# Where SyncE loads the rows of x and the tokens' values in a one-core cross-attention kernel

## The chip, the cores and the metric

The kernel runs on one core of a Trainium2 chip. The metric is the device time of one execution in microseconds. A core has TensorE (PE; its weight loads are listed as PEld), VectorE (DVE), ScalarE (ACT), GpSimd (POOL) and SyncE (SP). SP computes nothing here: it issues DMA transfers, one after the other in program order, and a transfer whose condition is not met holds up all transfers behind it on SP. POOL can issue transfers too, in its own order between its computations.

## The reference, cut to what matters

16 batches of 100 rows of x (640 wide), and for each a context of 722 rows (384 wide), of which the last 4 are extra tokens.

```python
query, keyt, valt = hidden_states @ Wq, enc @ Wk, enc @ Wv     # enc: 718 context rows
hs = _mha(query, keyt, valt)                                   # 8 heads of 80
ca_q1 = jnp.einsum('btc,th->bch', ca, Wq_ca)[:, indices, :]    # ca: the 4 tokens
ca_hs1 = _mha(ca_q1, residual, residual)                       # residual is x
ca_hs2 = _mha(ca_hs1 @ Wq, ca @ Wk_ca, ca @ Wv_ca)
out = (hs + ca_hs2) @ Wout + b_out + residual
```

So each row of the output needs, besides the main attention `hs`, a second small attention over the four tokens, whose values are `ca @ Wv_ca`, and at the very end the row of x itself.

## The kernel before, in words

Before the loop the kernel computes what all batches share. Among this are the tokens' values for all 64 tokens, written to a table `va_d` in DRAM (lines 1310 to 1327).

The loop (line 1346) goes over batches b = 0 to 15 and is software-pipelined. The order of all instructions on every engine is the order of the source (`manual_schedule`, line 1345); tiles come from pools with a fixed number of buffers, and the waits follow from who wrote and who read a buffer last. For batch b it runs, in TensorE's order:

- scores of b against the 718 keys (`s_ps`, line 716), three groups; ScalarE copies them to `st`, and DVE folds them into a running maximum `most` (lines 1392 and 1380). The last of these instructions is kept under the name `seen` (line 1401);
- a small product for the tokens' attention (`z_ps`, line 934);
- keys of batch b+1 and values of batch b from the context (`k_ps`, `v_ps`, lines 465 and 434). They are made by a scheme with fewer products: a bank of PSUM is filled, read by DVE or ScalarE (lines 405 and 407), and filled on top, so TensorE waits for these readings. `Maximum` (line 791) meanwhile turns `most` into one maximum per row: transpose (807), reductions, `spread` on ScalarE (829), transpose to `over` (837). Then `st - over` on DVE (1368) and the exponential on ScalarE (1376);
- the last fifth of the keys (`kT_ps`, 666); in some batches the output product (`o_ps`) of earlier rows or the queries of the next pair (`q_ps`);
- the product with V (`a_ps`, line 1585), 192 pairs of weight load and matmul in the trace, and the tokens' product `y_ps` (880) for a later batch. Then the next batch's scores.

The second attention is `Second` (line 859), mostly on POOL: `scores1` (four products and three sums of 100 x 800, waiting for `seen`), `scores2` (973), `softmax3` (987) and `values2` (line 992: `hs2`, the four tokens' values weighted, lines 1002 and 1009). For `values2` each of the four rows of `va_d` is spread over 100 partitions into a tile `vb` (250 KB); there are two such buffers. Tokens 0 and 1 are loaded by `Second.load`, **issued by POOL** (line 951, called at 1387, 1462, 1503 and 1559); tokens 2 and 3 by SP, each when the product on the buffer before it is done (line 1013).

`Last` (line 1023) finishes output rows. The 1600 rows are cut into 13 groups (`OC`). `Last.load` (line 1031) has SP load the rows of x of a finished group into `xn` (320 KB for 128 rows), and POOL adds the bias in place (1042). Pairs of groups are loaded in batches 3, 6, 8, 11 and 13 (line 1463). In the last batch three groups remain: `last.load()` (1531) for 128 rows and for 64 rows in two halves, `mine.load()` (1532) for the last 128 rows in a tile `spare`. `project_few` (1200) then multiplies the 64 rows by Wout, and DVE adds the result to `xn` (1213); the bigger groups follow at lines 1128 and 1122.

SP's order around the end of a batch is: tokens 2 and 3 (956); the next queries' rows and `ca` (203, 870); three loads of the context of batch b+2 (219); `mb` (843); two more of the context, `rest` (232), which wait for the last key product; then, in the batches named, `xn` (1041). As nothing holds these, they are issued while the product with V of the batch before runs.

Of the kernel before, what the change touches and what calls it, by code (L numbers as in the profile page):

```python
# [126 lines left out]
def kernel(  # L127
# [18 lines left out]
    nc = tc.nc  # L146
# [131 lines left out]
    for g in range(2):  # L278
        for c in range(CC):
            nc.scalar.dma_start(  # L280
                out=wv_sb[:, 2 * c + g],
                in_=wv[c * P : (c + 1) * P, g * (H // 2) : (g + 1) * (H // 2)],
# [42 lines left out]
    for h, c, r, s, k in PIECES:  # L325
        nc.gpsimd.dma_start(
            out=m2[s : s + k, c, h - HEADS[c][0], :T],
            in_=wqcat[h * D + r : h * D + r + k, :],
# [4 lines left out]
    for c in range(HC):  # L333
        first = c * P - HEADS[c][0] * D
        nc.gpsimd.affine_select(
            out=hmask[:, c], in_=hmask[:, c], compare_op=ALU.is_ge, fill=0.0,
# [3 lines left out]
            out=hmask[:, c], in_=hmask[:, c], compare_op=ALU.is_ge, fill=0.0,  # L340
# [439 lines left out]
    def wait_for(ins, other):  # L780

        tc.add_manual_dep(
            ins.ins,
            other.ins.name,
            mybir.DependencyInfo(
                mybir.DependencyClass.Sync, mybir.DependencyReason.DATA
            ),
            reason="apart",
        )
# [69 lines left out]
    class Second:  # L859
# [87 lines left out]
            )  # L947
            self.z = z

        def load(self):  # L950
            self.vb = [self.piece(nc.gpsimd, t) for t in range(2)]

        def piece(self, engine, t):
            b = self.b
            vb = vb_tile(f"vb_{b}_{t}")
            engine.dma_start(
                out=vb[:S], in_=va_d[b * T + t].unsqueeze(0).to_broadcast([S, H])
            )
            return vb

        def scores2(self, engine=nc.vector):
# [61 lines left out]
    class Last:  # L1023
# [4 lines left out]
            self.split = b == B - 1  # L1028
            self.t_ps = None

        def load(self):

            self.xn = {}
            for r, (lo, n) in enumerate(OC):
                if self.b != O_AFTER[r]:
                    continue
                xn = self.xn[r] = spare[1] if r == len(OC) - 1 else xn_tile(f"xn_{r}")
                rows = x.rearrange("b s n -> (b s) n")[lo : lo + n]
                for at, cols in self.parts(n):
                    to = xn[at : at + n, : cols.stop - cols.start]  # L1040
                    nc.sync.dma_start(out=to, in_=rows[:, cols])
                    nc.gpsimd.tensor_tensor(to, to, bias[at : at + n, cols], ALU.add)

        def parts(self, n):
# [201 lines left out]
    for n, heads in enumerate(HEADS):  # L1246
        cols = len(heads) * B * T
# [26 lines left out]
    second = Second(0, xT, ca_0)  # L1274
# [71 lines left out]
    for b in range(B):  # L1346
        p = b // 2
        e_in, now = enc, second
# [35 lines left out]

        if b == 0:
            enc_sums(enc)
            now.load()
            now.softmax1()
        st.append(scores(b, 0, tiles))
        if b == 0:  # L1390
# [15 lines left out]
        if b == 0:  # L1406
            second.scores1()
            m_next = load_m(b + 2)
            kk.go(3)
            top.go(3)  # L1410
            first_values(3, e_in, (act, act), get=bank)
            top.go(1)
            kk.go(2)
            now.scores2()
            now.exponentials2()
            first_values(0, e_in, (act, act), (0,), bank)
            top.go()
            kk.go(3)
            first_values(0, e_in, (act, act), (1,), bank)
            now.softmax3()  # L1420
            kk.go(2)
            subtract(0)
            exponential(0)
            kk.go(2)
            subtract(1)
            kk.go(3)
            exponential(1)
            second_next, enc_next = loads()
            less = subtract(2)
            exponential(2)  # L1430
            last_keys(b + 1, enc)
            enc_next = load_rest(b + 2, enc_next)
            keys(m_next)
            now.values2(less)
            enc_sums(enc_next)
            second.softmax1(4)
        elif b + 1 < B:
            vv = Values(b, e_in)

            def both(n):  # L1440
                vv.go(n)
                kk.go(n)

            forms = [wout_sb[:, 2 * i : 2 * i + 2, k * (H // 2) : (k + 1) * (H // 2)]
                     for i in range(2) for k in range(2)]
            if b == 2:
                for o, left, right in (
                    (forms[1], forms[1], forms[0]),
                    (wout2[:, 0], forms[3], forms[1]),
                    (wout2[:, 1], forms[2], wout2[:, 0]),  # L1450
                ):
                    nc.gpsimd.tensor_tensor(o, left, right, ALU.subtract)
            elif last.b - 1 in PAIRS:
                nc.gpsimd.tensor_tensor(wout2[:, 0], wout2[:, 0], forms[0], ALU.add)
            second.scores1(seen, range(T - 1))
            top.go(3)
            kk.go(3)
            vv.go(3)
            now.scores2(nc.gpsimd)
            second.scores1(None, range(T - 1, T))  # L1460
            if b == 1:
                now.load()
            last.load()
            top.go(1)
            if b > 1:
                last.place()
            now.exponentials2()
            both(2)
            both(2)
            top.go()  # L1470
            both(1)
            now.softmax3()
            if b == 1:
                nc.gpsimd.tensor_tensor(last.hs[:S], last.hs[:S], last.hs2, ALU.add)
            if last.b in PAIRS:
                last.sums()
            parted = b % 2 and b > 1 and last.b not in PAIRS
            now.values2(None, range(T - 1 if parted else T))
            vv.go(2)
            kk.go(1)  # L1480
            subtract(0)
            exponential(0)
            vv.go(1)
            subtract(1)
            vv.go(1)
            kk.go(2)
            exponential(1)
            vv.go(1)
            kk.go(2)
            both(1)  # L1490
            both(1)
            if b == 1:
                for f in list(wv_there):
                    nc.scalar.copy(wv_sb[:, W_AT[f]], wv_there.pop(f))
            mixed = None
            if b % 2 and b > 1:
                second_next, enc_next = loads()
                mixed = Queries(p + 1, xT_at[0], enc_next[0])
            if parted:
                mixed.sums()  # L1500
                now.values2(None, range(T - 1, T))
            else:
                second.load()
            if b == 1:
                nc.gpsimd.dma_start(out=bias, in_=bout[0].partition_broadcast(P))
            if not mixed:
                second_next, enc_next = loads()
            if b + 2 < B:
                m_next = load_m(b + 2)
            subtract(2)  # L1510
            exponential(2)
            last_keys(b + 1, enc)
            if b + 2 < B:
                enc_next = load_rest(b + 2, enc_next)
            if b == 1:
                last.transpose()
            if last.b in PAIRS:
                second.softmax1(3)
                last.project_pair()
                if last.b == max(PAIRS):  # L1520
                    nc.sync.dma_start(
                        out=forms[1],
                        in_=wout[: 2 * P, H // 2 :].rearrange("(c p) n -> p c n", p=P),
                    )
            second.softmax1(3 if parted else 8)
        else:
            room = enc_tile("spare").rearrange("p f k -> p (f k)")
            spare.extend(room[:, i * H : (i + 1) * H] for i in range(2))
            last.transpose()
            vv = Values(b, e_in)  # L1530
            last.load()
            mine.load()
            top.go(3)
            vv.go(3)
            last.project_few(len(OC) - 2)
            now.scores2(nc.gpsimd)
            now.exponentials2()
            top.go(1)
            vv.go(2)
            top.go()  # L1540
            vv.go(3)
            now.softmax3()
            now.values2()
            vv.go(2)
            subtract(0)
            exponential(0)
            vv.go(5)
            for i in (1, 2):
                subtract(i)
                exponential(i)  # L1550
            last.project()
        if b % 2 and b + 1 < B:
            xT, tiles = xT_at[0], queries_tiles(p + 1)
            if not mixed:
                for n in range(HC):
                    queries(p + 1, xT, tiles, n)
            elif parted:
                mixed.make(tiles, second.softmax1)
                second.load()
            else:  # L1560
                keys(m_next)
                mixed.sums()
                mixed.make(tiles, second.softmax1)
# [109 lines left out]
```

## Time and profile before

| what | value |
|---|---|
| device time, median of 3 runs | 924.46 us (923.11 to 924.51) |
| device time of the profiled execution | 922.65 us |
| its span, first to last instruction | 920.9 us |
| granted TensorE clock | 1.000 |
| transfers issued by POOL for `vb` | 32 |
| transfers issued by SP for `vb` | 32 |
| bytes moved, mean rate | 62.94 MB, 68 GB/s |

The profile is one execution, recorded instruction by instruction. In its timeline a row has the start and length in us, the engine, the source line, the operation, the tile written, the tiles read, shapes and the number of instructions merged; in brackets is the idle time of the engine before it and what ended it. A row of the table of windows has a stretch of time, its length, the busy time of each engine in it with the number of instructions, the granted clock, the busy share of the 16 DMA engines and the rate. Line numbers are those of the kernel before.

### The profile page before, as it was taken

To read this page: it belongs to the slowest core of one execution; us is meant where nothing else is said; L and a number is where in the kernel's file an instruction comes from. 1 tells how busy PE (TensorE), PEld (TensorE's weight loads), DVE (VectorE), ACT (ScalarE), POOL (GpSimd) and SP (SyncE) were. 2 spreads that over 40 slices of the span, in tenths; PEclk is the share of its full clock that TensorE was granted. 3 is DMA by queue.
4 is the path that set the end of the run, shared out by engine and by line. 5 is a ranking of instruction groups with operands and counts; after the bars stand their busy time and mean duration, and the time that the engine had idled before them with its cause. 6 is when DMAs were issued, how large, how long until landed. Compare 5 with 4: busy or idle time off the path is not lost.

```text
span 920.9 us, 27684 instructions
## 1 busy us (share of the span) xinstructions
PE 911.9 (99%) x11974; PEld 766.2 (83%) x11974; DVE 692.5 (75%) x1116; ACT 434.4 (47%) x836; POOL 723.6 (79%) x689
## 2 busy tenths in 40 slices
PE   9999999999999999999999999999999999999998
PEld 6988879787797979888798887988879888797966
DVE  3469895988649887795967869689784898748883
ACT  2234543737427373552737436264741737426341
POOL 5849999788977879697896969958798687976623
PEclk9999999999999999999999999999999999999999
DMA  8722013050300404031030410205030050310201
GB/s 270 269 77 78 25 49 95 1 156 2 104 32 11 119 1 134 3 97 60 24 111 3 117 40 30 77 2 155 3 101 33 2 157 1 104 46 3 81 23 38
DMA packets 49681, 62.94 MB, mean 68 GB/s; under 512 B 14072, under 2 KB 38200, under 8 KB 49560
## 3 DMA queue, kind: packets, MB, share of 16 engines
q1 hardware_dynamic: 45512, 51.49, 18.3%
q0 software_dynamic: 3024, 8.53, 3.0%
q8 instruction: 94, 1.54, 0.7%
q10 hardware_dynamic: 1024, 1.15, 0.4%
q14 instruction: 27, 0.22, 0.1%
HBM read 55.59 MB, written 5.57 MB: 66 GB/s over the span
## 4 chain that ended last, share of the span: by engine, by line
PE 97%; DVE 1%; DMA 0%; POOL 0%; issue 0%; ACT 0%; SPq 0%; ACTq 0%; POOLq 0%
PE s_ps L716 12%; PE a_ps L1585 11%; PE v_psA L434 11%; PE v_psB L434 9%; PE k_psA L465 8%; PE kT_ps L666 8%; PE k_psB L465 7%; PE o_ps L1160 5%; PE v_psC L434 4%; PE k_psC L465 3%; PE v_ps L375 2%; PE q_ps L593 2%; PE q_ps L535 2%; PE v_psD L434 2%; PE v_psE L434 2%; PE q_psA L593 1%
## 5 line engine op out<-in xcount | busy, mean ns | idle before, releaser
L905 POOL TENSOR_TENSOR e<-ca,g 100x800 f32<-100x800 f32 x64 | 99.4, 1564 | 91.8 <-ACT kT L407 64.3
L500 POOL TENSOR_TENSOR enc<-enc 128x240 f32<-128x240 f32 x135 | 106.6, 800 | 18.2 <-DMA enc<-in_enct 11.1
L1368 DVE TENSOR_TENSOR st<-st,over 120x1600 f32<-120x1600 f32 x48 | 113.8, 2373 | 0.0
L1585 PEld LDWEIGHTS a_ps<-vs,st 120*36 120x36 f32 (+3 forms) x3072 | 109.4, 124 | 3.9 <-issue 3.1
L1585 PE MATMUL a_ps<-vs,st 120*36 120x81 f32 (+3 forms) x3072 | 111.9, 233 | 0.3 <-ACT st L1376 0.3
L434 PE MATMUL v_psA<-wv_sb,enc 128*120 128x320 f32 x352 | 109.3, 433 | 0.0
L1009 POOL TENSOR_TENSOR hs<-hs,hs 100x640 f32<-100x640 f32 x48 | 96.3, 2007 | 3.8
L912 POOL TENSOR_TENSOR e<-e,e 100x800 f32<-100x800 f32 x48 | 92.1, 1919 | 3.8
L1002 POOL TENSOR_TENSOR hs<-vb,p 100x640 f32<-100x640 f32 x64 | 90.3, 1421 | 3.7 <-DMA vb<-va_d 0.9
L434 PE MATMUL v_psB<-wv_sb,enc 128*120 128x320 f32 x296 | 91.8, 433 | 0.0
L465 PE MATMUL k_psA<-enc,wk_sb 128*128 128x240 f32 x360 | 89.2, 370 | 0.0
L1376 ACT ACTIVATE st<-st 120x1600 f32<-120x1600 f32 x48 | 73.9, 1539 | 30.9 <-DVE st L1368 30.5
L434 PEld LDWEIGHTS v_psA<-wv_sb,enc 128*120 128x120 f32 x352 | 64.2, 183 | 25.0 <-DVE vs L405 0.5
L465 PEld LDWEIGHTS k_psA<-enc,wk_sb 128*128 128x128 f32 x360 | 67.2, 190 | 15.1
L1380 DVE TENSOR_TENSOR most<-most,st 120x800 f32<-120x800 f32 x64 | 67.3, 1052 | 15.5 <-ACT st L766 14.4
L716 PE MATMUL s_ps<-qp,kT 64*56 64x100 f32 (+1 forms) x3072 | 73.7, 248 | 0.6 <-issue 0.6
L465 PE MATMUL k_psB<-enc,wk_sb 128*128 128x240 f32 x300 | 73.0, 366 | 0.0
L716 PEld LDWEIGHTS s_ps<-qp,kT 64*56 64x56 f32 (+1 forms) x3072 | 67.1, 130 | 6.4 <-issue 5.2
L434 PEld LDWEIGHTS v_psB<-wv_sb,enc 128*120 128x120 f32 x296 | 54.1, 183 | 21.9 <-DVE vs L405 0.4
L1075 ACT COPY hsT<-turned_hs 32x160 f32<-32x160 f32 (+7 forms) x244 | 67.7, 278 | 3.0
L772 ACT COPY st<-s_ps 120x800 f32<-120x800 f32 x64 | 49.8, 829 | 34.3 <-PE s_ps L716 34.3
L465 PEld LDWEIGHTS k_psB<-enc,wk_sb 128*128 128x128 f32 x300 | 57.0, 190 | 7.7
(200 smaller groups left out, 1864.7 us busy)
## 6 DMA issues: line engine op xcount, KB each, us to landing
vb<-va_d POOLq DMA_DIRECT2D x32, 250.0 KB, 3.6
vb<-va_d SPq DMA_DIRECT2D x32, 250.0 KB
enc<-in_enct SPq DMA_DIRECT2D x30, 240.0 KB
enc<-in_enct SPq DMA_DIRECT2D x15, 360.0 KB
xT<-in_xt SPq DMA_DIRECT2D x8, 500.0 KB
rest<-in_enct SPq DMA_DIRECT2D x31, 120.0 KB
xn<-in_x SPq DMA_DIRECT2D x11, 320.0 KB
out<-xn SPq DMA_DIRECT2D x11, 320.0 KB
```

The source lines that it names most:

```text
L434: nc.tensor.matmul(at[0][j][:KN, : H // 2], a_form(self.enc, f)[:, j * KN : (j + 1) * KN], wv_there.get(f, wv_sb[:, W_AT[f]]), start=first ...
L465: nc.tensor.matmul(at[:, i * KT : (i + 1) * KT], wk_sb[:, W_AT[f], i], a_form(self.enc, f), start=(first and i == 0), stop=last, skip_grou ...
L500: nc.gpsimd.tensor_tensor(out, left, right, op)
L666: nc.tensor.matmul(bank[:, i * KT : (i + 1) * KT], weights[c], a_raw(enc, u, c), start=(i == 0 and c == 0), stop=(c == CC - 1), skip_group ...
L716: nc.tensor.matmul(s_ps[at][k0:k1, cols], w, rhs, start=not begun & {(at, k) for k in range(k0, k1, 32)}, stop=last, skip_group_check=True,)
L905: first = nc.gpsimd.tensor_tensor(to, self.ca[:, t, :].unsqueeze(1).to_broadcast([S, NH, S]), g[:, :, t].unsqueeze(2).to_broadcast([S, NH, ...
L912: nc.gpsimd.tensor_tensor(e, e, to, ALU.add)
L1002: first = nc.gpsimd.tensor_tensor(to, self.vb[t][:S].rearrange("p (h d) -> p h d", h=NH), p2[:, :, t].unsqueeze(2).to_broadcast([S, NH, D] ...
L1009: nc.gpsimd.tensor_tensor(sums, sums, to, ALU.add)
L1368: return nc.vector.tensor_tensor(st[i], st[i], top.over[:KN].unsqueeze(1).to_broadcast([KN, 2, ROWS]), ALU.subtract,)
L1376: nc.scalar.activation(st[i], st[i], AF.Exp, scale=SCALE)
L1585: nc.tensor.matmul(a_v[lo:hi, h % 4], st[i // 2][: KEYS[i], i % 2, h * S + lo : h * S + hi], block(i, h // 4)[: KEYS[i], h % 4], start=(i ...
```

## The change

The tokens' values of tokens 0 and 1 are issued by SP and not by POOL (POOL keeps batch 0), and in the batch that uses them instead of in the batch before. The first of them, and in batches 1 to 14 the rows of x as well, get a wait on `seen`, the last maximum over that batch's scores. In the last batch the rows of x get no wait of their own; their place in SP's order is behind the tokens' values. The bias addition keeps its place in POOL's order, and no computation is added or removed.

```diff
-        def load(self):
-            self.vb = [self.piece(nc.gpsimd, t) for t in range(2)]
-
-        def piece(self, engine, t):
+        def load(self, engine=nc.sync, behind=None):
+            self.vb = [self.piece(engine, t, behind) for t in range(2)]
+
+        def piece(self, engine, t, behind=None):
             b = self.b
             vb = vb_tile(f"vb_{b}_{t}")
-            engine.dma_start(
+            dma = engine.dma_start(
                 out=vb[:S], in_=va_d[b * T + t].unsqueeze(0).to_broadcast([S, H])
             )
+            if behind:
+                wait_for(dma, behind)
             return vb
...
-        def load(self):
+        def load(self, behind=None):
...
-                    nc.sync.dma_start(out=to, in_=rows[:, cols])
+                    dma = nc.sync.dma_start(out=to, in_=rows[:, cols])
+                    if behind:
+                        wait_for(dma, behind)
                     nc.gpsimd.tensor_tensor(to, to, bias[at : at + n, cols], ALU.add)
...
-            now.load()
+            now.load(nc.gpsimd)
...
-            if b == 1:
-                now.load()
-            last.load()
+            now.load(behind=seen)
+            last.load(seen)
...
-            else:
-                second.load()
             if b == 1:
                 nc.gpsimd.dma_start(out=bias, in_=bout[0].partition_broadcast(P))
...
             vv = Values(b, e_in)
+            now.load(behind=seen)
             last.load()
             mine.load()
...
                 mixed.make(tiles, second.softmax1)
-                second.load()
```

## The prediction

> **What bounds the kernel now.** I read the page first: busy times, DMA queues, then the chain that ended last.
>
> ```profile
> PE 911.9 (99%) x11974; PEld 766.2 (83%) x11974; DVE 692.5 (75%) x1116; ACT 434.4 (47%) x836; POOL 723.6 (79%) x689
> ...
> q8 instruction: 94, 1.54, 0.7%
> ...
> PE 97%; DVE 1%; DMA 0%; POOL 0%; issue 0%; ACT 0%; SPq 0%; ACTq 0%; POOLq 0%
> ```
>
> TensorE carries 97% of the chain, so no transfer is worth its own length: the change counts only where it alters a stall of TensorE. Batches repeat the same instructions, so stalls show when one stage is compared across batches. The table of windows does it, from the first product with V (a_ps) to the first key product after the next batch's scores. Columns: stretch, length, busy time (instructions) of PE, PEld, DVE, ACT, POOL, clock, DMA share, GB/s. The rows are the products of batches 2, 4, 10 and 12.
>
> ```profile
> 195.50:212.33 16.83, 15.78 (x518) 14.62 (x517) 11.88 (x23) 6.58 (x12) 12.68 (x19) 1.00 0.35 91
> 309.39:324.60 15.21, 15.21 (x518) 14.35 (x517) 11.03 (x22) 5.83 (x11) 12.69 (x19) 1.00 0.22 59
> 636.54:652.73 16.19, 15.42 (x517) 14.41 (x516) 11.43 (x22) 5.83 (x11) 11.78 (x19) 1.00 0.31 95
> 749.79:765.43 15.64, 15.47 (x517) 14.41 (x516) 11.37 (x21) 5.85 (x11) 12.02 (x19) 1.00 0.31 96
> ```
>
> Batch 4 has no idle time (15.21 of 15.21). Batches 2, 10 and 12 lose 1.62, 0.98 and 0.43 us. The timeline says where, with the idle time in brackets:
>
> ```profile
> 204.38 1.25 PE L716 MATMUL s_ps<-qp,kT 64*56 64x100 f32 x46 [0.47 <-issue]
> ...
> 211.95 0.45 PE L934 MATMUL z_ps<-y_sb,e 100*32 100x33 f32 x31 [0.58 <-issue]
> ...
> 644.73 0.52 PE L880 MATMUL y_ps<-m,xT 128*64 128x108 f32 x8 [0.77 <-POOL enc L500]
> ...
> 758.02 1.43 PE L716 MATMUL s_ps<-qp,kT 64*64 64x100 f32 x56 [0.17 <-issue]
> ```
>
> Three are "issue": waiting for nothing the profile shows. I take them for the loading of TensorE's own instructions. Queue q8 moved 1.54 MB in 94 packets, 16 KB each; 2 x 11974 TensorE instructions over 94 are 255 per packet. In this stage some 518 + 517 pass in 15.21 us: a packet is used up in 3.75 us, and the next must be there. Here are the transfers around batch 10's product: timeline, windows of 1 us, and the DMA view of 642.25 to 643.40 (packets, MB, share).
>
> ```profile
> 635.93 1.10 POOL L956 DMA_DIRECT2D vb<-va_d  x2
> ...
> 636.64 0.82 SPq L232 DMA_DIRECT2D rest<-in_enct  x2
> ...
> 637.51 0.90 SPq L1041 DMA_DIRECT2D xn<-in_x  x2
> ```
>
> ```profile
> 639.00:640.00 1.00, 1.00 (x35) 1.00 (x32) 0.96 (x2) 0.00 (x0) 0.62 (x1) 1.00 0.94 311
> ...
> 641.00:642.00 1.00, 1.00 (x34) 1.00 (x31) 0.97 (x3) 0.19 (x1) 0.48 (x1) 1.00 1.01 389
> ...
> 643.00:644.00 1.00, 0.96 (x28) 0.81 (x23) 0.79 (x3) 0.00 (x0) 1.00 (x3) 1.00 0.00 0
> ```
>
> ```profile
> q8 instruction: 1, 0.02, 5.4%
> ```
>
> The DMA engines are full (0.94 to 1.01) until just after 642; only as they empty does the instruction packet pass, and 1.3 us after that view's end TensorE resumes. Batches 2, 10 and 12 are those in which vb, rest and xn all load at the product's start. Batch 4 has vb and rest but no xn, share 0.22, and no stall. So I put 644.73 down to the same cause, not to POOL, which the wait names.
>
> **Part 1: loads out of the product.** vb (2 x 250 KB) and xn (2 x 320 KB) leave this stretch; rest stays. All 1.62 + 0.98 + 0.43 = **3.0 us** should go, the second stall of batch 2 being a consequence of the first. Bounds: 0 if rest alone delays the packet; 4.8 if the 1.81 us by which the median (924.46) exceeds the profiled execution (922.65) are stalls of this kind too. I take 3.0, the rows' own value.
>
> [...]
>
> **Part 2: POOL gives up 30 of its 32 issues.**
>
> ```profile
> L956 POOL DMA_DIRECT2D vb<-va_d x32: 537/555/627, 72.2 to 863.0; - x32
> ...
> DMA to landing us min/median/max: 3.2/3.6/5.4
> ```
>
> 30 x 0.555 = 16.7 us of POOL work go, worth nothing beyond Part 1: the only in-loop stall of TensorE on POOL is the 0.77 us counted there. SP takes the 30 issues, about 0.4 us each; it has the time:
>
> ```profile
> SPq L956 <- POOL hs L1002: 509.7, 32, 41.5
> ```
>
> **Part 3: the new wait, batches 1 to 14.** `seen` is the last maximum over the scores; the transpose of `most` follows it. SP now holds vb until then; behind vb stand xn, the tokens 2 and 3, and the next loads. The last two groups were already held by later work. Batch 11:
>
> ```profile
> 655.88 1.01 DVE L807 STREAM_TRANSPOSE turned<-most 128x800 f32<-128x800 f32 x1
> ...
> 668.27 3.05 POOL L1042 TENSOR_TENSOR xn<-xn,bias 128x640 f32<-128x640 f32 x2
> ```
>
> POOL first wants xn 12.4 us after `seen`, being busy with the next scores, and vb later still. Loads that need some 6 us (below) are hidden: 0 us. If that cover were gone, the whole 6 us would show. They now run beside key and value products, where an instruction packet lasts over 20 us (four value products, 888.03 below, take 1.24).
>
> **Part 4: the last batch, where the cover is gone.** There is no next batch, so POOL is idle. xn, its two halves and the last rows carry no wait there, but SP's order puts them behind vb, which waits. Before, they were loaded during batch 14:
>
> ```profile
> 850.78 1.53 SPq L956 DMA_DIRECT2D vb<-va_d  x2
> 852.40 1.60 SPq L1041 DMA_DIRECT2D xn<-in_x  x3
> ```
>
> ```profile
> 856.50:857.00 0.50, 0.50 (x4) 0.41 (x3) 0.49 (x2) 0.00 (x0) 0.49 (x1) 1.00 0.04 13
> 857.00:858.00 1.00, 1.00 (x6) 0.78 (x6) 1.00 (x2) 0.00 (x0) 1.00 (x1) 1.00 0.00 0
> ```
>
> The same five loads took from 850.78 to about 856.7, 5.9 us. What they release, across the engines:
>
> ```profile
> 863.54 3.33 POOL L1042 TENSOR_TENSOR xn<-xn,bias 128x640 f32<-128x640 f32 x3
> 866.95 1.55 POOL L1042 TENSOR_TENSOR spare<-spare,bias 128x640 f32<-128x640 f32 x1
> 886.17 0.24 POOL L973 TENSOR_TENSOR e<-s,mx 100x32 f32<-100x32 f32 x1 [17.68 <-DVE mx L971]
> 893.97 2.51 POOL L1002 TENSOR_TENSOR hs<-vb,p 100x640 f32<-100x640 f32 x2
> ```
>
> ```profile
> 878.74 2.01 DVE L1380 TENSOR_TENSOR most<-most,st 120x800 f32<-120x800 f32 x2
> ...
> 884.88 0.49 DVE L1213 TENSOR_TENSOR xn<-o_ps,xn 128x320 f32<-128x320 f32 x1 [0.64 <-issue]
> ...
> 886.15 0.82 DVE L405 TENSOR_TENSOR vs<-v_psA,vs 120x640 f32<-120x640 f32 x1
> ...
> 888.32 1.01 DVE L837 STREAM_TRANSPOSE over<-spread 128x800 f32<-128x800 f32 x1 [0.35 <-ACT spread L829]
> ...
> 896.95 0.82 DVE L405 TENSOR_TENSOR vs<-v_psB,vs 120x640 f32<-120x640 f32 x1 [0.30 <-PE v_psB L434]
> ```
>
> ```profile
> 886.58 1.71 ACT L829 COPY spread<-mx 64x800 f32<-64x800 f32 x2
> ```
>
> ```profile
> 888.03 1.24 PE L434 MATMUL v_psA<-wv_sb,enc 128*120 128x320 f32 x4
> ...
> 897.88 1.29 PE L1109 MATMUL o_ps<-wout_sb,hsT 128*128 128x320 f32 x4
> ```
>
> `seen` is 878.74 + 2.01 = 880.75. The five loads are issued from 880.8. In batch 14 the second vb came 1.2 us after the first; here it comes 0.4 after, 0.8 sooner, so they land at X between 880.8 + 5.1 and + 5.9; I take **X = 886.5**. (Outer bounds: the fifth is issued about 882.6, two vb at 0.4 and xn's parts at 0.5 later than 880.8, and a vb load took 3.2 to 5.4 us: 885.8 to 888.0.) POOL then adds the bias: 3.33 us, so DVE L1213, which reads those rows, starts at X + 3.4 = 889.9, not 884.88. POOL's fourth addition ends at X + 5.0; L973 stands behind it, 891.5 instead of 886.17. ScalarE's exponential waits for L973 and stands ahead of the spread; `over` came 888.32 - 886.17 = 2.15 us after L973, so it comes at X + 7.2 = 893.7: **+5.4 us** (4.7 to 6.9). DVE executes in order: behind `over` stand the readings of the value banks (L405), the first subtraction, and the reading at 896.95 that frees a bank for the o_ps product at 897.88. TensorE cannot refill a bank before DVE reads it, so DVE's short waits for TensorE in this run shift too. Nothing absorbs the 5.4 us, and all that follows the o_ps product shifts by it. vb itself, wanted at 893.97, is in time.
>
> **The sum:** 922.65 - 3.0 + 0 + 5.4 = **925.05 us** against the profiled execution (span 920.9 plus 1.75 around it). On the median, 1.81 us higher, it is 924.46 + 2.4 = **926.9 us**.
>
> **Rivals**, on the median. *More stalls than the profile holds:* the runs' extra 1.81 us are instruction stalls too, the gain is 4.8, the sum +0.6: 925.1. For it: the run times scatter over 1.4 us; against it: eleven products show none. *Faster:* the same mechanism further. It decides from a gain of 5.4 + 1.85 = 7.3 us, so from about four more stalls of 1.0 us (the mean of 1.62, 0.98 and 0.43): -1.9, 922.5. Against it: that exceeds the 1.81 us. *No gain:* rest and the context loads hold the instruction packet as long, and only the tail counts: 924.46 + 5.4 = 929.9. For it: rest is issued within 0.9 us of the others; against it: batch 4. [...] *A slower clock:* TensorE's product at 888.03 waits for the reading at 886.15, which comes 5.0 us later and ends at 892.0: 4.0 us idle. If the clock then halves for the two products that TensorE can do before DVE sets the pace again, 1.24 us each, up to 2.5 us are added: 929.4. The rows shown have clock 1.00 throughout, and no such gap. [...] *The change not doing what it says* has no chance of its own: the 30 loads stand in SP's order.
>
> **How the numbers follow.** A measurement can tell about 0.2% (1.85 us) from no change. Forecast 926.9: 0.42. More stalls, within 0.2%: 0.30. Faster: 0.13. No gain: 0.10. Clock: 0.05. Slower is 0.42 + 0.10 + 0.05 = 0.57. The range goes from -1.0 us (gain 6.4; beyond it lies most of "faster") to the no-gain case, 923.5 to 929.9, and leaves out less than 0.2. The forecast alone, X from 885.8 to 888.0, spans 926.2 to 928.4.
>
> **What would show it.** Windows of the products of batches 2, 10 and 12 at 15.2 us show Part 1; at 15.6 to 16.8, "no gain". POOL L1042 in batch 11 waiting for DMA breaks Part 3. In the last batch, POOL L1042 some 5.8 us after `seen` and waiting for DMA, `over` 12.9 us after `seen` (7.6 now), and a TensorE gap of about 4 us after the v_psE product show Part 4; L1213 at its old distance from `seen` (4.1 us) would make the forecast wrong.

## The result and the profile after

| | before | after |
|---|---|---|
| device time, median of 15 runs each | 923.11 us (920.39 to 925.47) | 928.04 us (924.62 to 930.85) |
| the profiled execution | 922.65 us, span 920.9 | 924.62 us, span 922.9 |
| granted TensorE clock of the profiled execution | 1.000 | 0.998 |

The ratio is 1.0051, 95% interval 1.0036 to 1.0066. A second set of runs of the same kernel (below, e7) gave 926.85 against 923.92 us, 1.0031 (1.0014 to 1.0047). The change makes the kernel slower by 0.3 to 0.5%.

The page of the kernel after, busy times. It says little: POOL has 30 instructions and 18.8 us less (723.6 before), and TensorE's busy time is the same.

```profile
PE 911.7 (99%) x11974; PEld 766.2 (83%) x11974; DVE 701.6 (76%) x1116; ACT 434.5 (47%) x836; POOL 704.8 (76%) x659
```

The stages say more. Table of windows of the kernel after, the products with V of batches 2, 10 and 12 (the row of batch 4, 15.21 us as before, is not shown):

```profile
194.74:209.95 15.21, 15.21 (x517) 14.35 (x517) 12.14 (x22) 5.82 (x11) 11.96 (x18) 1.00 0.10 25
...
634.12:649.33 15.21, 15.21 (x517) 14.35 (x516) 11.18 (x22) 5.82 (x11) 11.94 (x18) 1.00 0.09 23
746.42:761.63 15.21, 15.21 (x517) 14.35 (x517) 11.17 (x22) 5.82 (x11) 11.96 (x18) 1.00 0.09 22
```

Length equals PE's busy time in all of them: the stalls of 1.62, 0.98 and 0.43 us are gone, and the DMA share fell from about 0.33 to 0.10. The last batch gives back more than that. Timeline of the kernel after (line numbers moved by a few: L1384 was L1380, L1046 was L1042, L1217 was L1213, L1113 was L1109):

```profile
874.71 2.01 DVE L1384 TENSOR_TENSOR most<-most,st 120x800 f32<-120x800 f32 x2
876.79 0.73 SPq L956 DMA_DIRECT2D vb<-va_d  x2
877.88 1.57 SPq L1043 DMA_DIRECT2D xn<-in_x  x3
...
883.15 3.27 POOL L1046 TENSOR_TENSOR xn<-xn,bias 128x640 f32<-128x640 f32 x3 [24.74 <-DMA xn<-in_x]
886.46 0.49 DVE L1217 TENSOR_TENSOR xn<-o_ps,xn 128x320 f32<-128x320 f32 x1 [6.26 <-POOL xn L1046]
...
887.59 0.81 DVE L405 TENSOR_TENSOR vs<-v_psA,vs 120x640 f32<-120x640 f32 x1
...
888.46 1.84 PE L434 MATMUL v_psA<-wv_sb,enc 128*120 128x320 f32 x4 [4.30 <-DVE vs L405]
...
890.15 1.01 DVE L837 STREAM_TRANSPOSE over<-spread 128x800 f32<-128x800 f32 x1 [0.82 <-ACT spread L829]
...
900.10 5.60 PE L1113 MATMUL o_ps<-wout_sb,hsT 128*128 128x320 f32 x20
```

`seen` is 874.71 + 2.01 = 876.72. Read the chain by its brackets: SP issues the loads behind `seen` (vb, xn, and spare right after); POOL, idle for 24.74 us, waits for the DMA; DVE waits 6.26 us for POOL; TensorE waits 4.30 us for DVE's reading of v_psA. From `seen` to the o_ps product it is now 23.38 us; before it was 897.88 - 880.75 = 17.13: **+6.25 us**. The same four product matmuls at 888.46 take 1.84 us and not 1.24, and the table of windows shows why in its PEclk column (the first of the last three):

```profile
888.00:890.00 2.00, 1.54 (x4) 1.05 (x5) 1.23 (x2) 1.71 (x3) 0.24 (x2) 0.79 0.36 82
890.00:892.00 2.00, 2.00 (x5) 1.27 (x4) 1.78 (x3) 0.12 (x1) 0.00 (x0) 0.50 0.00 0
892.00:894.00 2.00, 2.00 (x7) 1.26 (x7) 1.92 (x5) 0.75 (x2) 0.00 (x0) 0.86 0.00 0
```

The clock drops to half behind the gap, for (0.21 x 2 + 0.50 x 2 + 0.14 x 2) / 0.50 = 3.4 us. It sets in at 890.00 - 0.21 x 2 / 0.50 = 889.16, 0.7 us after TensorE has resumed.

Part 3 of the prediction is seen in batch 11, same kernel, timeline: vb is issued at `seen` (652.46) and xn 0.8 us behind it, and POOL's addition, 12.4 us after `seen` as before, has no bracket, so it waits for nothing.

```profile
653.28 0.83 SPq L1043 DMA_DIRECT2D xn<-in_x  x2
...
664.88 3.04 POOL L1046 TENSOR_TENSOR xn<-xn,bias 128x640 f32<-128x640 f32 x2
```

### The profile page after: what moved, and what is told of

Same layout as the page of the kernel before. It is cut to its first block, busy times and chain, and to the rows that moved or that the text cites. A ratio compares the mean times of both kernels' runs of the same rounds, so it can differ in the third digit from the quotient of the medians.

```text
span 922.9 us, 27705 instructions
## 1 busy us (share of the span) xinstructions
PE 911.7 (99%) x11974; PEld 766.2 (83%) x11974; DVE 701.6 (76%) x1116; ACT 434.5 (47%) x836; POOL 704.8 (76%) x659
## 4 chain that ended last, share of the span: by engine, by line
PE 97%; DMA 1%; DVE 1%; POOL 0%; issue 0%; ACTq 0%; SPq 0%; POOLq 0%
PE s_ps L716 12%; PE a_ps L1586 12%; PE v_psA L434 10%; PE v_psB L434 9%; PE k_psA L465 8%; PE kT_ps L666 8%; PE k_psB L465 7%; PE o_ps L1164 5%; PE v_psC L434 4%; PE k_psC L465 3%; PE v_ps L375 2%; PE q_ps L593 2%; PE q_ps L535 2%; PE v_psD L434 2%; PE v_psE L434 2%; PE q_psA L593 1%
## 5 line engine op out<-in xcount | busy, mean ns | idle before, releaser
L1380 ACT ACTIVATE st<-st 120x1600 f32<-120x1600 f32 x48 | 73.9, 1539 | 32.0 <-DVE st L1372 31.3
L1384 DVE TENSOR_TENSOR most<-most,st 120x800 f32<-120x800 f32 x64 | 65.9, 1030 | 16.6 <-ACT st L766 15.5
```

What stands on the lines that cost most here:

```text
L1380: nc.scalar.activation(st[i], st[i], AF.Exp, scale=SCALE)
```

## The experiments

The theory: the loss is the last batch's wait alone, and the loop gains some 3 to 4 us. The rival: moving the loads costs something inside batches 1 to 14 as well. e1 and e2 separate the two halves of the change; e3 and e4 split its gain; e5, e8 and e9 test what makes a stall; e6 and e7 size the tail. Times are medians, each beside runs of the kernel before on the same chip.

**e1, the rows ahead of the values.** The changed kernel with one line of the last batch moved:

```diff
-            now.load(behind=seen)
             last.load()
             mine.load()
+            now.load(behind=seen)
```

> The changed kernel, but in the last batch the rows of x stand ahead of the tokens' values in SP's order, as they did before the change. Theory, that the loss is the last batch's wait: L1217 and `over` come as long after `seen` as before (4.1 and 7.6 us), TensorE has no idle time of 4 us and stays at clock 1.000, and the gains in the loop remain: 3.8 to 4.5 us faster than the kernel before, 918.5 to 919.5 us against a median of 923.1. Rival, that waits or transfers inside batches 1 to 14 cost what was gained in the products: the run stays within 1 us of the changed kernel, 927 to 928. Between them, 921 to 922: the gain of 4.3 us that the two profiles show is larger than what the other executions have.

Measured: 919.83 against 923.49 us, 0.9966 (0.9953 to 0.9978), 3.7 us faster than the kernel before. Timeline of e1:

```profile
875.86 2.00 DVE L1384 TENSOR_TENSOR most<-most,st 120x800 f32<-120x800 f32 x2
...
881.97 0.49 DVE L1217 TENSOR_TENSOR xn<-o_ps,xn 128x320 f32<-128x320 f32 x1 [0.61 <-issue]
...
894.97 5.60 PE L1113 MATMUL o_ps<-wout_sb,hsT 128*128 128x320 f32 x20
```

L1217 starts 4.1 us after `seen` (877.86), as before, and the o_ps product 17.11 us after it (17.13 before): the tail is back to what it was. The rival inside the loop falls. The stalls are not quite zero here: products of batches 2 and 4 took 15.57 and 15.72 us, with waits of TensorE called "issue", and rest the only one of the three loads beside them.

**e2, the last batch alone.** The kernel before, with only this: the load in batch 14 is left to the last batch, and goes to SP there (not shown: `load` takes the engine and the wait as arguments, as in the change).

```diff
-            else:
+            elif b < B - 2:
                 second.load()
...
             vv = Values(b, e_in)
+            now.load(nc.sync, seen)
             last.load()
```

> The kernel before, with only the last batch as in the change: SP loads tokens 0 and 1 behind `seen`, ahead of the rows of x. Theory, that the wait of the last batch costs about 6 us by itself and the drop of the clock behind it 1 to 2 us more: 6 to 8 us slower than the kernel before, 929 to 931, with the stalls in the products of batches 2 and 10 still there and one stretch of half clock behind a TensorE gap of about 4 us. Rival, that the wait is hidden as long as the loop keeps its old order: within 1 us of the kernel before, 922 to 924.

Measured: 930.77 us, 1.0083 (1.0069 to 1.0098). Its products of batches 2, 10 and 12 keep their stalls (windows), and its tail is that of the kernel after (timeline):

```profile
194.59:210.69 16.10, 15.77 (x518) 14.62 (x517) 11.12 (x22) 6.03 (x12) 11.79 (x19) 1.00 0.33 95
...
635.74:651.60 15.86, 15.42 (x518) 14.42 (x517) 10.92 (x22) 5.83 (x11) 11.89 (x19) 1.00 0.33 97
749.01:764.91 15.90, 15.47 (x517) 14.41 (x516) 11.06 (x22) 5.85 (x11) 12.02 (x19) 1.00 0.33 96
```

```profile
878.00 2.01 DVE L1382 TENSOR_TENSOR most<-most,st 120x800 f32<-120x800 f32 x2
...
889.71 0.49 DVE L1215 TENSOR_TENSOR xn<-o_ps,xn 128x320 f32<-128x320 f32 x1 [6.21 <-POOL xn L1044]
...
903.35 2.91 PE L1111 MATMUL o_ps<-wout_sb,hsT 128*128 128x320 f32 x10
```

Its loop is that of the kernel before up to batch 13, so the two profiles show how far one execution can be trusted: batches 2, 4, 10 and 12 took 16.83, 15.21, 16.19 and 15.64 us there and 16.10, 15.72, 15.86 and 15.90 here. The stall of a single product is known to some 0.7 us only.

From `seen` (880.01) to o_ps 23.34 us, +6.21. The two halves add up: -0.34% (e1) and +0.83% (e2) make +0.49%, and the whole change was measured at +0.51 and +0.31%.

**e3, the rows alone,** and **e4, the values alone.** The kernel before, with one of the two groups of loads held until `seen`. e3 leaves the last batch as it was (not shown: the argument of `Last.load`, as in the change). e4 has the load function of the change and its place in the loop, and the last batch of e1, where the rows stand ahead of the values:

```diff
-            last.load()
+            last.load(seen)
```

> The kernel before, with only the rows of x held until `seen` in batches 1 to 14; the tokens' values stay on POOL and in the product. Theory, that what holds up TensorE's instructions is the sum of transfers started at the head of the product, of which the rows are the largest: the products of batches 10 and 12 fall to 15.2 us, 1.4 to 3 us faster than before, about 920 to 921.5, no gap in the last batch. Rival, that the tokens' values are what delays the instructions (or POOL's issues): the products keep 16.2 and 15.6 us and the time stays within 0.7 us of before.

```diff
-            if b == 1:
-                now.load()
             last.load()
+            now.load(behind=seen)
```

> The kernel before, with only the tokens' values moved to SP and held until `seen`; the rows of x are loaded as before, ahead of them in SP's order, in the last batch too. Theory, that the sum of transfers at the head of a product decides and not one of them: the products of batches 2, 10 and 12 lose most of their stalls, 1.4 to 3.5 us faster than before, 919.5 to 921.5, no gap in the last batch. Rival, that the rows alone fill the DMA engines long enough: the products of batches 10 and 12 keep their 16.2 and 15.6 us, only batches 0 to 2 gain, 1 to 2 us.

Measured: e3 921.17 us, 0.9979 (0.9969 to 0.9989); e4 919.77 us, 0.9965 (0.9952 to 0.9978). The products of batches 2, 10 and 12 are 15.21 us long in both; here are the windows of batch 10, first e3, then e4:

```profile
635.74:650.95 15.21, 15.21 (x517) 14.35 (x516) 11.04 (x22) 5.82 (x11) 12.87 (x19) 1.00 0.20 57
```

```profile
634.75:649.96 15.21, 15.21 (x517) 14.35 (x516) 11.40 (x22) 5.81 (x11) 12.02 (x18) 1.00 0.23 67
```

Taking away either half of the load takes away all three stalls; both rivals fall. e1 holds both halves and gained no more than e4. In e3 POOL still issues every load it issued before, and the stall of batch 10 whose wait named POOL is gone too. The tile `m` that the waiting product reads had been written by POOL at 638.97, 5.8 us before TensorE resumed. POOL was not the cause.

**e5, more loads.** The kernel before, with two more loads of 320 KB in four products, into a scratch table:

```diff
                 enc_next = load_rest(b + 2, enc_next)
+            if b in (2, 4, 10, 12):
+                for k in range(2):
+                    nc.sync.dma_start(
+                        out=dram.tile([P, H], F32, name=f"extra_{b}_{k}"),
+                        in_=x.rearrange("b s n -> (b s) n")[k * P : (k + 1) * P],
+                    )
```

> The kernel before, with two more loads of 128 rows of x (320 KB each, into a scratch table that nobody reads) issued by SP behind `rest` in the products of batches 2, 4, 10 and 12. Theory, that transfers at the head of a product hold up TensorE's instructions: the product of batch 4, 15.21 us without a stall, becomes 15.6 to 16.8 us as the three others were, and those three stall longer, 1 us more each or so: 2 to 5 us slower than the kernel before. Rival, that the stalls belong to something else in those batches (POOL, whom one of the waits names): batch 4 keeps its 15.2 us, and the time stays within 1 us.

Measured: 923.03 against 923.92 us, 0.9988 (0.9973 to 1.0002): the theory's 2 to 5 us did not come. Windows of the products of batches 2, 4, 10 and 12:

```profile
194.85:211.39 16.54, 15.76 (x517) 14.62 (x516) 11.86 (x22) 6.58 (x12) 12.00 (x19) 1.00 0.41 133
308.45:323.90 15.45, 15.41 (x518) 14.47 (x517) 11.26 (x22) 6.06 (x12) 12.47 (x19) 1.00 0.34 104
635.81:651.54 15.73, 15.43 (x518) 14.42 (x517) 11.28 (x22) 5.83 (x11) 11.81 (x19) 1.00 0.45 140
748.96:765.41 16.45, 15.69 (x518) 14.50 (x517) 11.78 (x22) 6.36 (x12) 11.68 (x19) 1.00 0.43 132
```

Batch 4, now with a burst like that of batch 10 (though the extra loads go to DRAM and not to `xn`), has 0.24 us of stall; e1, e2 and e3 had 0.51 there without them. With twice the rows batches 2 and 10 are 0.3 and 0.5 us shorter than before, within the scatter, and batch 12 is 0.8 us longer. The 1 us more that the theory gave each of them came in one of three, so the amount of transfers alone does not size a stall. Windows of 1 us of e5 in batch 10, and the DMA view of 641.20 to 642.30:

```profile
641.00:642.00 1.00, 1.00 (x36) 1.00 (x33) 0.86 (x3) 0.87 (x1) 0.92 (x2) 1.00 0.64 255
642.00:643.00 1.00, 1.00 (x35) 1.00 (x30) 0.86 (x2) 0.00 (x0) 1.00 (x2) 1.00 1.02 394
```

```profile
q8 instruction: 1, 0.02, 5.5%
```

TensorE's instruction packet passed here in a dip of the burst (0.64), and the engines were full again (1.02) behind it. It does not wait for the end of the whole burst.

**e8 and e9, the same loads, other blocks.** Set against TensorE's instructions started by then (24148 in all, 200 of them neither matmul nor weight load), the arrivals of q8's 94 packets lie along a line of 256.1 instructions per packet in the trace of the kernel before, and of 256.0 in that of the kernel after; with 156 instructions more e8 has 95 packets, with 52 more e9 has 94. If a stall needs such a block of 256 to begin inside the burst, moving the blocks against the loads must move the stalls. The kernel before with 39, or 13, tiny matmuls of zeros ahead of everything, 156 or 52 TensorE instructions:

```diff
         nc.tensor.matmul(idle_ps[:, :P], idle, idle, start=True, stop=True)
+    for _ in range(39):
+        nc.tensor.matmul(idle_ps[:32, :4], idle[:, :32], idle[:, :4], start=True, stop=True)
```

> The kernel before, with 39 tiny matmuls of zeros (156 TensorE instructions) ahead of its first products, and not one load moved. It shifts the ends of the blocks of 256 instructions by 100 instructions, which in a product with V is 1.5 us later. Theory, that a stall arises where a new block is begun while the transfers at the product's head are still running, so that the fetch of the block after it has to wait for them: the blocks now begin closer to the end of the burst, and the stalls of batches 2, 10 and 12 vanish (15.2 us, save small ones of under 0.3 us), 2 to 3 us off, minus what the matmuls cost at the start (up to 2). Rival, that the amount of transfers alone decides, or POOL: 16.8, 16.2 and 15.6 us stay.

> The kernel before, with 13 tiny matmuls of zeros (52 TensorE instructions) ahead of its first products, and not one load moved. The blocks of 256 instructions then end 52 instructions earlier, 0.75 us in a product with V. Theory, that the fetch of the next block waits for the end of the burst of transfers, whenever its block began: the stalls of batches 2, 10 and 12 grow by up to 0.75 us each, products of about 17.5, 16.9 and 16.4 us, 1 to 2 us slower than the kernel before. Rival: 16.8, 16.2 and 15.6 us stay, the time within 0.7 us.

Measured: e8 928.31 against 923.36 us, 1.0060 (1.0046 to 1.0074); e9 926.34 us, 1.0032 (1.0019 to 1.0044). The times say little, since the tiny matmuls cost more than was allowed for (78 passes took 4.32 us at the start of e8, and the first batch's key and value stage another 2.2 us). The products do: batches 2, 4, 10 and 12, first e8, then e9.

```profile
201.53:217.06 15.53, 15.48 (x517) 14.49 (x516) 9.73 (x18) 5.82 (x11) 10.92 (x18) 1.00 0.36 100
314.66:330.70 16.04, 15.89 (x518) 14.71 (x517) 10.99 (x22) 5.82 (x11) 11.93 (x19) 1.00 0.22 57
643.43:659.52 16.09, 15.40 (x517) 14.43 (x516) 11.72 (x22) 6.70 (x12) 12.42 (x19) 1.00 0.33 97
756.59:771.80 15.21, 15.21 (x518) 14.35 (x517) 11.08 (x22) 5.83 (x11) 12.58 (x19) 1.00 0.34 101
```

```profile
198.21:214.59 16.38, 15.41 (x518) 14.44 (x517) 10.91 (x22) 5.83 (x11) 12.31 (x19) 1.00 0.34 94
...
639.99:656.00 16.01, 15.75 (x517) 14.68 (x516) 12.06 (x22) 5.82 (x11) 12.64 (x19) 1.00 0.33 97
753.06:769.47 16.41, 15.59 (x517) 14.56 (x516) 11.24 (x22) 5.89 (x11) 11.82 (x19) 1.00 0.33 94
```

With no load moved, e8 rid batch 12 of its stall at full load (DMA share 0.34), took 1.3 us from batch 2, and gave batch 4, with vb and rest only (0.22), a stall of 0.83 us. e9 added 0.77 us to batch 12, as expected, but took 0.4 and 0.2 from batches 2 and 10, which were to grow. Much of this is no larger than the scatter between the kernel before and e2. Clearer are two products that no other profile delays: batch 5 of e8 and batch 3 of e9 (windows).

```profile
370.76:386.49 15.73, 15.39 (x521) 14.41 (x517) 8.96 (x15) 5.57 (x10) 10.20 (x15) 1.00 0.08 26
```

```profile
264.51:280.20 15.69, 15.38 (x520) 14.40 (x517) 8.04 (x13) 5.28 (x10) 8.40 (x11) 1.00 0.01 3
```

In the nine profiles without padding both products take 15.16 or 15.17 us, and each padded kernel has the other's batch at 15.16. So padding alone makes and moves stalls, which the rival denies and which the position of the blocks would explain. But e9's theory, that the fetch waits for the burst's end, does not give the sizes, and these two stalls have hardly a load beside them (DMA shares 0.08 and 0.01). Batch 10 of e8 keeps 0.88 us; 0.69 of them stand at 659.34, and the DMA view of 655.7 to 659.4 holds two packets, both of instructions. That stall has no data transfer beside it at all; its cause stays open.

**e7, the changed kernel again,** and **e6, with TensorE kept busy.** e7 is unaltered. e6 has six matmuls of 128x320 more in the gap, into a bank that nobody reads:

```diff
-            vv.go(3)
+            vv.go(1)
+            warm = psumk("warm")
+            for _ in range(6):
+                nc.tensor.matmul(
+                    warm[:, : H // 2], ident, wv_sb[:, 0], start=True, stop=True
+                )
+            vv.go(2)
```

> The changed kernel unaltered, profiled a second time, as the baseline of the runs beside it: its median lay 4.9 us above that of the kernel before, its profiled execution only 2.0 us. If the profiled execution was one with a cheap tail, this profile shows more than the 6.25 us by which the last value stage grew (two stretches of half clock in place of one, or a longer TensorE gap) and the same products at 15.2 us. Rival: the tail is the same 6.25 us, and the products show stalls that the first profile did not have.

> [...] The time at which DVE's reading lets TensorE go on is not altered. Theory, that the half clock behind the gap is a cost of its own: clock 1.000, no half-clock window, and 1.8 us less than the changed kernel (0.5 of 3.41 us), about 926 against 928. Rival, that DVE sets the pace behind the gap and TensorE's slowness is hidden: clock 1.000 and within 0.5 us of the changed kernel.

Measured: e7 926.85 us, 1.0031 (1.0014 to 1.0047); e6 926.76 us, 1.0028 (1.0014 to 1.0042). Timeline of e7, and its windows behind the gap:

```profile
877.53 2.01 DVE L1384 TENSOR_TENSOR most<-most,st 120x800 f32<-120x800 f32 x2
...
889.54 0.49 DVE L1217 TENSOR_TENSOR xn<-o_ps,xn 128x320 f32<-128x320 f32 x1 [6.51 <-POOL xn L1046]
...
891.54 2.49 PE L434 MATMUL v_psA<-wv_sb,enc 128*120 128x320 f32 x4 [4.55 <-DVE vs L405]
...
904.27 2.10 PE L1113 MATMUL o_ps<-wout_sb,hsT 128*128 128x320 f32 x7
```

```profile
890.00:892.00 2.00, 0.46 (x1) 0.46 (x2) 1.86 (x5) 0.64 (x2) 1.32 (x2) 0.59 0.22 51
892.00:894.00 2.00, 2.00 (x5) 1.16 (x5) 1.18 (x2) 1.19 (x2) 0.00 (x0) 0.50 0.14 31
894.00:896.00 2.00, 2.00 (x6) 1.16 (x5) 1.84 (x4) 0.00 (x0) 0.00 (x0) 0.50 0.00 0
896.00:898.00 2.00, 2.00 (x7) 1.32 (x6) 1.77 (x4) 0.58 (x2) 0.50 (x1) 0.70 0.00 0
```

Timeline of e6, whose clock stays at 1.000:

```profile
878.46 2.01 DVE L1384 TENSOR_TENSOR most<-most,st 120x800 f32<-120x800 f32 x2
...
887.75 3.39 PE L1546 MATMUL warm<-wv_sb,ident 128*128 128x320 f32 x12
...
891.13 0.49 DVE L1217 TENSOR_TENSOR xn<-o_ps,xn 128x320 f32<-128x320 f32 x1 [7.18 <-POOL xn L1046]
...
893.12 1.34 PE L434 MATMUL v_psA<-wv_sb,enc 128*120 128x320 f32 x4 [1.98 <-DVE vs L405]
...
896.27 1.34 PE L434 MATMUL v_psC<-wv_sb,enc 128*120 128x320 f32 x4 [0.73 <-DVE vs L405]
...
904.31 2.10 PE L1113 MATMUL o_ps<-wout_sb,hsT 128*128 128x320 f32 x7
```

The tail of each profile, split at L1217, from the rows shown:

| kernel | `seen` to L1217 | L1217 to o_ps | sum against before | half clock |
|---|---|---|---|---|
| before | 4.13 us | 13.00 us | | none |
| e1 | 4.11 | 13.00 | -0.02 us | none |
| after | 9.74 | 13.64 | +6.25 | 3.4 us |
| e2 | 9.70 | 13.64 | +6.21 | 3.4 us |
| e7 | 10.00 | 14.73 | +7.60 | (0.41 + 0.50 + 0.50 + 0.30) x 2 / 0.50 = 6.8 us |
| e6 | 10.66 | 13.18 | +6.71 | none |

The first column is the loads; it varies by 1 us from execution to execution. The second is the clock: without half clock (e6, one execution) only 0.18 us remain of it, where DVE is late once (0.73). So half clock costs an estimated 0.5 to 1.6 us of each execution profiled. In the medians it can't be seen: e6 gained 0.1 us over e7, not the 1.8 of the theory, but the intervals are 1.3 us either way, and in its profile the loads happened to land latest. The times settle neither theory. The granted clock of whole executions says a little more: of the 27 runs of the changed kernel, 14 have 0.998, as one stretch of 3.4 us gives, with a median of 926.8 us, and 13 have 0.996, as 6.8 us give, with 928.3. A later landing lengthens both the wait and the gap, so not all of these 1.5 us need be the clock.

## Why the prediction was right

**Part 1 was right in size, and in cause only by half.** The three products went to 15.21 us (15.24, 15.21 and 15.27 in e7). The loop's gain, measured without the tail, is 3.1 us by the ratio of e1 (2.0 to 4.3) and 3.2 by that of e4: the 3.0 us of the rows, not the 4.8 of "more stalls". That the loads at the product's head made these three stalls is shown: without padding, the three products lose 0.4 to 1.6 us each in every profile with the full burst (before, e2, e5), and at most 0.07 us in the six with a thinner one, save 0.36 in batch 2 of e1. Either half of the burst can go (e3, e4).

How the loads do it was given as "only as they empty does the instruction packet pass", and that is only half true. e5's packet passed in a dip inside the burst, doubled loads clearly lengthened one stall of three, and e8 and e9 made stalls in other batches without moving a load. That the stalls are late blocks of instructions is argued from the late packet and from the padding; how the loads and the position of a block act together is open. The prediction also counted eleven products without a stall, and two of them were not: in its own profile batch 0 took 16.04 us and batch 13 15.61 (15.21 and 15.46 in the kernel after).

**Part 2 was right:** POOL lost 30 issues and 18.8 us (16.7 predicted), and no wait of TensorE in the loop was POOL's to shorten. By their ratios e3, where POOL keeps its issues, gained 1.9 us and e4 3.2; the intervals overlap, so a worth of POOL's time beyond the stalls is not shown. **Part 3 was right:** POOL's only wait for `xn` is the 24.74 us of the last batch, TensorE has no new wait in batches 1 to 14, and e1 and e4, which keep their new waits, are the fastest kernels of the study.

**Part 4 was right in mechanism and too small in size.** Its chain came true link by link (SP behind `seen`, POOL waiting for DMA, L1217, the v_psA reading, the gap in TensorE). The mis-sized term is X: L1046 was to start 5.75 us after `seen` and started 6.43 us after it (883.15 - 876.72), and the first column of the table ranges from 9.70 to 10.66 us where the prediction had 9.15. `over` came 13.4 us after `seen`, 12.9 were predicted, and the gap was 4.30 us, 4.0 predicted. To the +5.4 us, X adds 0.6 to 1.5 and the clock 0.5 to 1.6 where it drops, and 0.2 that the sum had too much go off: 6.2 to 7.6 us in the profiles. By e2's ratio the last batch costs 7.7 us (6.4 to 9.1).

**The clock was a rival with a chance of 0.05; it came in every profile in which the gap was left open (after, e2, e7).** It came in all 32 runs of the changed kernel and of e2 as well: their granted clock is 0.998 or 0.996, and 0.999 or 1.000 in every run of the kernel before whose clock is on record. The prediction had estimated the gap at 4.0 us and still left the clock out of its sum; that the clock would halve was a supposition, which no row of the profile before showed. The runs show 3.4 us of half clock behind gaps of 4.25 to 4.30 us, twice that in e7 behind 4.55, and none in e6 where 1.98 us were left. How long a gap must be is not shown beyond these, nor what sets the moment: in the kernel after the drop came 0.7 us after TensorE had resumed (889.16 and 888.46).

**The sum** was 0.26% above its baseline (926.9 over 924.46, +2.4 us); +0.51 and +0.31% were measured (4.9 and 2.9 us between the medians). As a time it came closer, beside medians of 928.04 and 926.85. That is luck: the kernel before now ran 0.5 to 1.4 us below 924.46, which covers part of what the tail was short. The profiled execution of the kernel after was the fastest of its 15 runs. e7's span is 4.2 us longer, 1.35 of it in the tail, and some 2.0 in products with V that took a little longer. The largest are 0.66 us in the product of batch 0 and 0.50 in that of batch 11, where hardly anything is loaded (DMA share 0.02; windows of e7):

```profile
701.27:716.95 15.68, 15.38 (x521) 14.40 (x517) 8.03 (x13) 5.27 (x10) 8.40 (x11) 1.00 0.02 3
```

Such delays come and go between executions of one kernel. What sets them is open.

## What to carry to other kernels

Here a load moved behind a wait delayed everything that stood behind it in the same queue (the last batch's xn, with no wait of its own, was issued at 877.88 us in the kernel after, 1.16 us behind `seen`, and at 852.40 in the kernel before): find the batch, here the last, in which the work that used to hide it is missing, and there put the loads without a wait first (e1: one line moved turned +0.5% into -0.3%). Where TensorE loses a few tenths of a microsecond to "issue" in some batches and not in others, compare what loads beside them: here thinning out one burst was enough for the largest stalls. Smaller ones came and went with no load beside them, and instructions added elsewhere moved them, so take more than one profile before naming a cause. A gap in TensorE of 4.3 us cost more than its length here, by an estimated 0.5 us, since the clock halved for 3.4 us behind it; one filled up to 2.0 us had no half clock behind it (e6).

## What was not expected of the hardware

- Doubling the rows loaded in a burst (DMA share of the product up from about 0.32 to 0.43) lengthened TensorE's stall clearly in one batch of three (0.8 us). With tiny matmuls of 156 and 52 TensorE instructions at the start of the program, batches 5 and 3 had stalls of 0.57 and 0.53 us; in nine profiles without them these batches had none.
- A wait of 0.69 us on "issue" (e8, 659.34) with no data packet on any DMA engine in the 3.6 us before it.
- Half clock of 6.8 us behind one gap of 4.55 us, and of 3.4 us behind one of 4.30.
